# Two cross-attention layers: the order in which a score tile's readers follow each other, and value rows and Gram matrix read back from memory

## The chip, the cores and the metric

One core of a Trainium2 chip runs the whole kernel. The metric is the device time of one execution in microseconds. The core has a matrix engine (TensorE), a vector engine (VectorE), an activation engine (ScalarE), a general engine (GpSimd) and a queue that issues transfers (SyncE); in the profile they are PE (PEld for weight loads), DVE, ACT, POOL and SP. Each engine works through its own instructions in order, and engines wait for each other through semaphores.

## The reference

Two layers of cross-attention follow each other, each with a residual. x is 64 x 256 x 320, the context 64 x 77 x 512; there are 20 heads of 16 channels.

```python
# layer 0: 77 text tokens (the image part is empty)
q, k, v = heads(x @ Wq.T), heads(ctx @ Wk.T), heads(ctx @ Wv.T)
x = merge(softmax(q @ k.T / 4) @ v) @ Wo.T + bo + x

# layer 1: 73 text tokens, and the last 4 as image tokens
q, k_t, v_t = heads(x @ W_q), heads(text @ W_k), heads(text @ W_v)
probs_t = softmax(q @ k_t.T / 4)
text_out = probs_t @ v_t
qsem = l2norm(probs_t @ text)                 # 512 wide
sem = qsem @ l2norm(ip).T
probs_ip = softmax(q @ k_ip.T / 4 + 0.5 * sem) * spatial_mask
x = (text_out + probs_ip @ v_ip) @ W_out + b_out + x
```

## The kernel before, in words

Everything is float32. Channels lie on the partitions for x, queries and outputs; tokens of x lie on the partitions for scores. A pair p of batches (32 pairs) is the unit of projections and outputs. The attention of one layer and one pair is cut into ten units: for each of the two batches b five units of 8 heads by 128 tokens (`UNITS`). One iteration g of the main loop handles one unit of layer 0 (pair p = g // 10, kind k = g % 10), and one unit of layer 1 that lies 13 iterations back (`LAG`), so that layer 1 of pair p - 1 runs with layer 0 of pair p. The loop runs for 345 iterations; layer 0 ends with g = 319.

**The scores' tile.** `sc` takes four of the eight PSUM banks and has one buffer. In each iteration TensorE writes three things into it: the semantic products of a layer 1 unit (`semantics`, L774 and L781), the scores of the layer 0 unit and the scores of the next layer 1 unit (`scores`, L659). The semantic products multiply the unnormalised layer 1 weights with a block of columns: the Gram matrix of the context (77 columns), the value columns and a column of ones. So one product gives, per head, the dot products with the context that norm and image similarity need, the text output and the sum of the weights.

Readers of `sc` in an iteration: VectorE takes the maximum of each head's scores (L677) and the difference to it (L679), for layer 0 and then layer 1 (`shifted`); VectorE multiplies the Gram part with the weights (`weighted`, L792 and L795), whose sum (L1130) is the squared norm; ScalarE copies the last columns out (`sums_out`, L1057). The next iteration's `semantics` waits until all have read.

**What follows.** ScalarE takes the exponentials: layer 0 in L687 (`exponential(0)`), layer 1 in L690 and L691, which go to the tile `parts`. For layer 0, VectorE sums (L705) and inverts, and GpSimd multiplies (L710, tile `parts`). In the next iteration TensorE transposes both layers' weights (`transposed`, L723, L724; tile `tr`, two buffers for all of them, with `itr` and `ltr`), and ScalarE copies the transposes out: L730, L731 for layer 1; L749, L750, or L738, L741 for the last four heads, for layer 0. Layer 1's copies feed the next `semantics`; layer 0's feed the value products `attend` (L809, L814), after units 1 and 4 of a batch.

**Fillers.** `fillers(k, p)` lays the other work between these steps, by kind of iteration: projections of queries (`queries`, L547, L557; copied by L602), keys (`keys`, L345; copied by L348), value rows (`value_rows`, L390), output projections (`project`, L547, L557, added by VectorE in L617; `project_last`, L632, L636), the Gram matrix (`gram`, L512), the image weights' transposes (`image_transposed`, L915) and the outputs' transposes (`outputs`, L928, L940). They share the two buffers of tile `ms`. The list `first` lies between layer 1's and layer 0's transposes, `second` and `third` behind the iteration's vector work. `keep_order` keeps the order of the program on TensorE, VectorE, ScalarE and GpSimd throughout, and on SyncE for the first 13 iterations.

**The order in an iteration.** Scores; maxima and differences; image maximum (`middle`); transposes of layer 1 with their copies; exponential of layer 0 (for k = 5 later); `first`; the product; transposes of layer 0; the sums' copy (for k = 1 and 6 ahead of those transposes); exponentials of layer 1; normalising. For k = 2 `first` lies ahead of the product.

**Values and Gram.** `value_rows(i, l)` makes 128 rows of values of layer l; ScalarE copies them to `vs`, whose two layers go to a tile in memory with one transfer. `values(l, p, b)` reads a batch's rows back, piece by piece where they straddle row tiles: the first 64 tokens twice (`vm`), the remaining 13 or 9 eight times (`vr`, `v_rest`). `place_values` puts them on GpSimd into the block of columns (`gv`, `gr`), for layer 1 with 6 copies and 8 masked products. `gram` copies the Gram matrix from PSUM with two ScalarE copies, scales two parts on GpSimd, and doubles it with one transfer and eight small ones from SBUF to SBUF (L521, L525); `place_gram` spreads it into `gv` and `gr`.

**Tail.** After the last unit of layer 0, `keep_busy` lets TensorE make products that nobody reads (L759), 14 in most iterations with a layer 1 unit.

Of the kernel before, what the change touches and what calls it, by code (L numbers as in the profile page):

```python
# [31 lines left out]
QR = 32  # L32
SLOTS = H + 4
# [37 lines left out]
def tile_two_cross_attentions(ctx: ExitStack, tc: tile.TileContext, a: dict, out: bass.AP):  # L71
# [190 lines left out]
    for sign in (1, -1):  # L262
        nc.gpsimd.affine_select(
            out=rest1, in_=rest1, pattern=[[-sign * QR, 4], [-sign * R1, 2]], compare_op=ALU.is_ge,
            fill=0.0, base=0 if sign > 0 else R1 - 1, channel_multiplier=sign,
        )
# [20 lines left out]
    v_rest = [const.tile([P, C], F32, tag=f"v_rest{b}", name=f"v_rest{b}") for b in range(2)]  # L287
    g_rest = [const.tile([P, R0], F32, tag=f"g_rest{b}", name=f"g_rest{b}") for b in range(2)]
    for t in (*v_rest, *g_rest):
        nc.vector.memset(t, 0.0)  # L290
# [6 lines left out]
    v_rows = {}  # L297
# [83 lines left out]
    stage = {}  # L381

    def value_rows(i, l):

        n = min(P, NB * T - i * P)
        if l == 0:
            stage[i] = sp.tile([P, 2, C], F32, tag="vs", name=f"vs{i}", bufs=1)
        ps = pms.tile([P, 512], F32, tag="ms", name=f"v_ps{l}_{i}")
        for k in range(KE):
            nc.tensor.matmul(ps[:n, :C], cfs[i][:, k, :n], wv[l][:, k, :], start=(k == 0), stop=(k == KE - 1))  # L390
        nc.scalar.copy(stage[i][:n, l, :], ps[:n, :C])
        if l:
            v_rows[i] = dram.tile([P, 2, C], F32, tag="v_rows", name=f"v_rows{i}", bufs=8)
            nc.sync.dma_start(v_rows[i][:n], stage[i][:n])
            if (i + 2) * P < NB * T:
                load_rows(i + 2)

    def from_rows(to, l, p, b, t0, t1):

        r0 = (2 * p + b) * T  # L400
        at, end = r0 + t0, r0 + t1
        while at < end:
            i, r = divmod(at, P)
            n = min(P - r, end - at)
            o = at - r0 - t0
            nc.sync.dma_start(to[o : o + n, :], v_rows[i][r : r + n, l, :])
            at += n
# [5 lines left out]
    def values(l, p, b):  # L413

        nt = (T, TT)[l]
        rem = nt - M
        vm = small.tile([P, C], F32, tag="vm", name=f"vm{l}_{p}_{b}", bufs=1)
        vr = v_rest[b] if l else small.tile([8 * rem, C], F32, tag="vr", name=f"vr{p}_{b}", bufs=1)
        for e in range(2):
            from_rows(vm[e * M : (e + 1) * M, :], l, p, b, 0, M)  # L420
        for i in range(8):
            r = i // 2 * QR + i % 2 * rem if l else i * rem
            from_rows(vr[r : r + rem, :], l, p, b, M, nt)
        fetched[l] = (vm, vr)

    def place_values(l, p, b):
# [3 lines left out]
        if l:  # L430

            for j in range(2):
                rows = slice(j * M, (j + 1) * M)
                for part in range(2):
                    nc.gpsimd.tensor_copy(
                        gv[b][rows, part, :, T : T + D].rearrange("p (e a) d -> p e a d", e=2),
                        vm[rows, 8 * D * part : 8 * D * (part + 1)].rearrange(
                            "p (a j e d) -> p j e a d", a=2, j=2, e=2
                        )[:, j],
                    )  # L440
                nc.gpsimd.tensor_copy(
                    gv[b][rows, 2, :, T : T + D].rearrange("p (e a) d -> p e a d", e=2),
                    vm[rows, HT * D + j * QR : HT * D + (j + 1) * QR]
                    .rearrange("p (e d) -> p e d", e=2).unsqueeze(2).broadcast_to([M, 2, 2, D]),
                )
            for r in range(4):
                rows = slice(r * QR, (r + 1) * QR)
                full = [QR, 2, 2, D]
                nc.gpsimd.tensor_tensor(
                    gr[b][rows, :2, :, T - M : T - M + D],  # L450
                    vr[rows, : HT * D].rearrange("p (i r e d) -> p r i e d", i=2, r=4, e=2)[:, r],
                    rest1[rows].unsqueeze(1).unsqueeze(3).broadcast_to(full), ALU.mult,
                )
                c0 = HT * D + r % 2 * QR
                nc.gpsimd.tensor_tensor(
                    gr[b][rows, 2, :, T - M : T - M + D], vr[rows, c0 : c0 + QR].rearrange("p (e d) -> p e d", e=2),
                    rest1[rows].unsqueeze(2).broadcast_to([QR, 2, D]), ALU.mult,
                )
            return
# [41 lines left out]
    grams = {}  # L501

    def gram(p, b):

        ct = cts[p]
        ps = pms.tile([P, 512], F32, tag="ms", name=f"g_ps{p}_{b}")  # L510
        for k in range(KE):
            nc.tensor.matmul(ps[:TT, :T], ct[:, k, b, :TT], ct[:, k, b, :], start=(k == 0), stop=(k == KE - 1))  # L512
        r = rip[:TT, (2 * p + b) * NIP : (2 * p + b + 1) * NIP]
        g = small.tile([P, T], F32, tag="gram", name=f"gram{p}_{b}", bufs=2)
        rows = small.tile([TT, R0], F32, tag="gram_rest", name=f"gram_rest{p}_{b}", bufs=2)
        nc.scalar.copy(g[:M, :M], ps[:M, :M])
        nc.scalar.copy(rows, ps[:TT, M:T])
        nc.gpsimd.tensor_mul(rows[:, R1:], rows[:, R1:], r)
        nc.gpsimd.tensor_scalar_mul(g[:M, M:TT], rows[:M, :R1], 2.0)
        nc.gpsimd.tensor_copy(g[:M, TT:], rows[:M, R1:])  # L520
        nc.sync.dma_start(g[M:, :], g[:M, :])  # L521
        gx = g_rest[b]
        for i in range(8):
            r0 = i // 2 * QR + i % 2 * R1
            nc.sync.dma_start(gx[r0 : r0 + R1, :], rows[M:TT, :])  # L525
        grams[b] = g

    def place_gram(b):
        g, gx = grams[b], g_rest[b]
# [166 lines left out]
    def rests(two):  # L696

        r = two[:, 4].rearrange("p j (a c) -> p (j a) c", c=QR)
        return r[:, :, : 2 * R1].rearrange("p r (e t) -> p r e t", e=2)
# [252 lines left out]
    def fillers(k, p):  # L952
# [18 lines left out]
        elif k == 1:  # L971
# [5 lines left out]
            add(1, p - 1, place_gram, 0)  # L977
            add(1, p, keys_by_head, 0, p, 1)
            add(1, p - 1, keys_by_head, 1, p - 1, 0)
        elif k == 2:  # L980
# [6 lines left out]
            add(2, p - 1, lambda: made["q"]())  # L987
            add(1, p - 1, place_values, 1, p - 1, 0)
# [21 lines left out]
        elif k == 6:  # L1010
# [9 lines left out]
            add(1, p, place_image_keys, p)  # L1020
            for b in range(2):
# [39 lines left out]
    for g in range(NP * NU + LAG + 12):  # L1061
# [22 lines left out]
        ends = before1 and before1[2] == BU - 1  # L1084
        for l in range(2):
# [11 lines left out]
        if k == 2:  # L1097
            for fn, args in first:
                fn(*args)
        if before1:  # L1100
            prod = weighted(ps, *before1[:4])
        if k != 2:
            for fn, args in first:
                fn(*args)
        if before1 and k in (1, 6):
            sums_out(ps)
# [3 lines left out]
        if idle > 2:  # L1110
            keep_busy(14 if now[1] else {13: 12, 14: 16, 15: 14, 16: 16, 17: 16}.get(idle, 0))
# [6 lines left out]
        if before1 and k not in (1, 6):  # L1118
            sums_out(ps)
# [84 lines left out]
```

## Time and profile before

| | |
|---|---|
| median of three runs | 2474.95 us (2473.02 to 2475.86) |
| the profiled execution | 2474.45 us, span 2472.7 us |
| granted TensorE clock, mean | 0.999 |
| busy: TensorE, VectorE, ScalarE, GpSimd | 97%, 80%, 60%, 55% |
| chain that ended last: TensorE, VectorE, ScalarE, transfers, GpSimd | 76%, 12%, 3%, 3%, 2% |
| layer 0 maximum, difference (each of 320) | 796 and 800 ns |
| layer 1 maximum, difference (each of 320) | 756 and 800 ns |
| product, both parts (each of 320) | 681 and 223 ns |
| sums' copy (each of 320) | 301 ns |
| exponential of layer 0 (each of 320) | 719 ns |
| one pair in the middle, k = 0 to k = 0 | 72.8 us (1179.42 to 1252.23) |

A row of the time line has the start, the duration, the engine, the line and operation, output and inputs, how many instructions are merged in it, and in brackets the idle time just before with what ended it. A row of the waits says which engine at which line waited for whom: total, times, longest. Instructions on one engine overlap a little in their recorded times, so the time from a start to the next start is often less than the duration.

### The profile page before, as it was taken

The page shows a single profiled execution, that of the slowest core. Times are in us where ns is not written, and L with a number is a line of the kernel's source. Part 1 is how long each engine was busy: PE and PEld are TensorE (multiplying, and loading weights), DVE is VectorE, ACT ScalarE, POOL GpSimd, SP SyncE. Part 2 cuts the span into 40 slices and gives each one's busy share as a digit, 9 for nine tenths or more (in the row PEclk, how much of TensorE's full clock was granted, in tenths as well). Part 3 has the DMA queues.
Part 4 walks back from the last instruction along what each step waited for, and adds up shares of the span by engine and source line. Part 5 has one row for each costly group of instructions (what it writes and reads, how often), then busy time and mean ns, then how long its engine had stood idle before and what let it go on. Part 6 is the DMA issues. An engine that isn't in the chain of part 4 may idle for free.

```text
span 2472.7 us, 100470 instructions
## 1 busy us (share of the span) xinstructions
PE 2394.2 (97%) x41118; PEld 1847.9 (75%) x41118; DVE 1987.4 (80%) x3673; ACT 1482.2 (60%) x3767; POOL 1370.9 (55%) x3483
## 2 busy tenths in 40 slices
PE   7899999999999999999999999999999999999888
PEld 5677777777777777777777777777777777777676
DVE  3588788888888888888888888888888888888864
ACT  3466666666666666666665666665665666666543
POOL 2455565566555656555656555556555556555542
PEclk9999999999999999999999999999999999999999
DMA  6212111112111112111121211121211121211000
GB/s 173 75 30 57 50 52 47 56 53 58 52 57 41 54 54 59 52 52 51 47 59 56 62 45 48 46 60 56 62 44 48 47 59 56 61 39 39 26 23 25
DMA packets 150914, 131.83 MB, mean 53 GB/s; under 512 B 45432, under 2 KB 129144, under 8 KB 150456
## 3 DMA queue, kind: packets, MB, share of 16 engines
q1 hardware_dynamic: 149592, 124.27, 17.5%
q8 instruction: 325, 5.32, 0.9%
q10 hardware_dynamic: 864, 1.15, 0.2%
q14 instruction: 133, 1.09, 0.1%
HBM read 87.43 MB, written 33.91 MB: 49 GB/s over the span
## 4 chain that ended last, share of the span: by engine, by line
PE 76%; DVE 12%; ACT 3%; DMA 3%; POOL 2%; issue 1%; SPq 1%; DVEq 0%; POOLq 0%; ACTq 0%
PE tr L723 10%; PE sc L774 9%; PE o_ps L547 8%; PE q_ps L547 8%; PE sc L659 7%; DVE w L679 5%; PE v_ps L390 4%; PE sc L781 4%; PE o_ps L632 3%; DVE mx L677 3%; PE k_ps L345 3%; PE pv L809 2%; PE q_ps L557 2%; PE o_ps L557 2%; PE q_ps L575 2%; PE pv L814 2%
## 5 line engine op out<-in xcount | busy, mean ns | idle before, releaser
L677 DVE TENSOR_REDUCE mx<-sc 128x8 f32<-128x584 f32 (+1 forms) x640 | 496.6, 776 | 342.1 <-PE sc L659 339.3
L710 POOL TENSOR_TENSOR parts<-w,sm 128x512 f32<-128x512 f32 (+1 forms) x640 | 440.6, 709 | 437.1 <-DVE sm L706 144.2
L679 DVE TENSOR_TENSOR w<-sc,mx 128x616 f32<-128x616 f32 x640 | 511.8, 800 | 73.0 <-DVE mx L677 1.4
L723 PE MATMUL tr<-ident,parts 128*128 128x128 f32 x2560 | 407.5, 282 | 9.5 <-ACT pt L730 5.6
L730 ACT COPY pt<-tr 128x512 f32<-128x512 f32 x320 | 187.1, 585 | 323.8 <-PE tr L723 318.9
L723 PEld LDWEIGHTS tr<-ident,parts 128*128 128x128 f32 x2560 | 284.2, 140 | 128.6 <-issue 83.1
L687 ACT ACTIVATE w<-w 128x616 f32<-128x616 f32 x320 | 230.1, 719 | 143.7 <-DVE w L679 142.7
L774 PEld LDWEIGHTS sc<-gv,pt 64*64 64x64 f32 x10240 | 233.5, 133 | 105.6 <-ACT sums L1057 52.7
L774 PE MATMUL sc<-gv,pt 64*64 64x94 f32 x10240 | 277.9, 245 | 23.6 <-ACT sums L1057 23.0
L694 POOL COPY att<-w 128x32 f32<-128x32 f32 x320 | 67.0, 209 | 354.6 <-DVE w L679 350.8
L705 DVE TENSOR_REDUCE sm<-w 128x8 f32<-128x616 f32 x320 | 250.9, 784 | 13.9 <-ACT w L687 13.8
L659 PE MATMUL sc<-kbd,q 32*64 32x154 f32 x10240 | 247.7, 293 | 1.1 <-ACT q L602 1.0
L547 PE MATMUL q_ps<-x,wq 128*128 128x256 f32 x1024 | 232.9, 380 | 5.3 <-ACT kT L348 5.3
L547 PE MATMUL o_ps<-aT,wo 128*128 128x256 f32 x1024 | 231.8, 379 | 0.7 <-ACT aT L945 0.7
L1057 ACT COPY sums<-sc 128x168 f32<-128x168 f32 x320 | 96.2, 301 | 225.8 <-DVE prod L795 223.9
L1130 DVE TENSOR_REDUCE nrm<-prod 128x8 f32<-128x584 f32 x320 | 226.7, 709 | 0.3
L792 DVE TENSOR_TENSOR prod<-sc,parts 128x512 f32<-128x512 f32 x320 | 217.9, 681 | 2.8 <-PE sc L781 2.8
L547 PEld LDWEIGHTS q_ps<-x,wq 128*128 128x128 f32 x1024 | 189.2, 190 | 30.2 <-ACT kT L348 7.3
L547 PEld LDWEIGHTS o_ps<-aT,wo 128*128 128x128 f32 x1024 | 189.6, 190 | 24.4 <-ACT aT L945 1.1
L690 ACT ACTIVATE parts<-w 128x512 f32<-128x512 f32 x320 | 206.4, 645 | 0.0
L749 ACT COPY pt<-tr 128x512 f32<-128x512 f32 x256 | 150.3, 587 | 66.9 <-PE tr L723 65.5
L390 PE MATMUL v_ps<-wv,cf 128*128 128x320 f32 (+1 forms) x624 | 179.2, 433 | 0.0
(144 smaller groups left out, 4560.3 us busy)
## 6 DMA issues: line engine op xcount, KB each, us to landing
out_dram<-x SPq DMA_DIRECT2D x64, 256.0 KB
x<-in_x_dram SPq DMA_DIRECT2D x31, 512.0 KB
v_rows<-vs SPq DMA_DIRECT2D x38, 320.0 KB
vm<-v_rows SPq DMA_DIRECT2D x152, 80.0 KB
ct<-in_ctx_dram SPq DMA_DIRECT2D x32, 308.0 KB
cf<-in_ctx_dram SPq DMA_DIRECT2D x38, 256.0 KB
g_rest<-gram_rest SPq DMA_DIRECT2D x512, 0.5 KB
v_rest<-v_rows SPq DMA_DIRECT2D x448, 11.2 KB
```

What stands on the lines that cost most here:

```text
L390: nc.tensor.matmul(ps[:n, :C], cfs[i][:, k, :n], wv[l][:, k, :], start=(k == 0), stop=(k == KE - 1))
L547: nc.tensor.matmul(ps[b][:, m, :], w[:, k, m * P : (m + 1) * P], main[:, k, b * S : (b + 1) * S], start=(k == 0 and m == 0), stop=False,)
L659: nc.tensor.matmul(ps[c, r, 2 * T * l : 2 * T * (l + 1)], tokens[rows, c], kbd[rows, part].rearrange("p e t -> p (e t)"), start=start, sto ...
L677: nc.vector.tensor_reduce(mx, sc[:, :, :, :nt], AX.X, ALU.max)
L679: nc.vector.tensor_tensor(w, sc, mx.unsqueeze(3).broadcast_to([P, 4, 2, T]), ALU.subtract)
L687: nc.scalar.activation(w, w, AF.Exp, scale=SCALE)
L705: nc.vector.tensor_reduce(sm, w, AX.X, ALU.add)
L710: nc.gpsimd.tensor_tensor(two[:, 8 * t0 : 8 * t1].rearrange("p (h t) -> p h t", h=8), w[:, :, t0:t1], sm.unsqueeze(2).broadcast_to([P, 8, ...
L723: nc.tensor.transpose(ps[:, i, :], flat[:, i * P : (i + 1) * P], ident)
L774: nc.tensor.matmul(ps[c, i % 2 * 2 + j, at : at + GV], pt[half_rows, i, c], gv[b][half_rows, part, i, :], start=start and i < 2, stop=False,)
L792: nc.vector.tensor_tensor(prod[:, :, :, :M], sm[:, :, :, :M], w[:, :4].rearrange("p (e a) j t -> p (a j) e t", e=2), ALU.mult)
L1130: nc.vector.tensor_reduce(eight(stats[q, b][2], u), prod, AX.X, ALU.add)
```

## The change

Three things. First, in each iteration the product and then the sums' copy come ahead of the maxima, with no exceptions by kind left; `first` follows the layer 0 exponential for every k. Second, the value rows go to two tables in memory, one for each layer, from which broadcast transfers read the repeated rows; layer 1's table holds the columns in the order in which `gv` and `gr` want them, so that placing takes one copy and one product; its remaining rows are read in slots of 16 tokens in place of 9, with the mask `rest1` and the layout `rests` changed to match. The Gram matrix goes to memory and comes back by two broadcast transfers (`gram_out`), and `place_gram` of batch 0 moves from k = 1 to k = 2. Third, 8 unread products in place of 14 in the tail.

```diff
+ER = QR // 2
...
     def value_rows(i, l):
...
+        rows = sp.tile([P, (C, 4 * 3 * QR)[l]], F32, tag=f"vs{l}", name=f"vs{l}_{i}", bufs=1)
+        if l == 0:
+            nc.scalar.copy(rows[:n], ps[:n, :C])
+            nc.sync.dma_start(v0_rows[r0 : r0 + n], rows[:n])
+            return
+        to = rows[:n].rearrange("p (r i c) -> p r i c", r=4, i=3)
+        nc.scalar.copy(
+            to[:, :, :2].rearrange("p r i c -> p i r c"), ps[:n, : 2 * P].rearrange("p (i r c) -> p i r c", i=2, r=4)
+        )
+        nc.scalar.copy(
+            to[:, :, 2].rearrange("p (s r) c -> p s r c", s=2),
+            ps[:n, 2 * P : C].rearrange("p (r c) -> p r c", r=2).unsqueeze(1).broadcast_to([n, 2, 2, QR]),
+        )
+        nc.sync.dma_start(v1_rows[r0 : r0 + n], rows[:n])
...
     def values(l, p, b):
...
+            for j in range(2):
+                nc.sync.dma_start(
+                    vm[j * M : (j + 1) * M].rearrange("p a i e d -> p a (i e d)"), rows[r0 : r0 + M, j::2]
+                )
+            for r in range(4):
+                src = rows[r0 + M : r0 + M + ER, r].unsqueeze(0)
+                nc.sync.dma_start(
+                    vr[r * QR : (r + 1) * QR].rearrange("p i c -> p (i c)"), src.broadcast_to([2, ER, 3 * QR])
+                )
+        else:
...
+            for to, t0, t1, n in ((vm, 0, M, 2), (vr, M, T, 8)):
+                src = v0_rows[r0 + t0 : r0 + t1].unsqueeze(0)
+                nc.sync.dma_start(to, src.broadcast_to([n, t1 - t0, C]))
...
     def place_values(l, p, b):
...
+            nc.gpsimd.tensor_copy(
+                gv[b][:, :, :, T : T + D].rearrange("p i (e a) d -> p i e a d", e=2),
+                vm.rearrange("p a i e d -> p i e a d"),
+            )
+            nc.gpsimd.tensor_tensor(
+                gr[b][:, :, :, T - M : T - M + D], vr.rearrange("p i (e d) -> p i e d", e=2),
+                rest1.unsqueeze(1).unsqueeze(3).broadcast_to([P, 3, 2, D]), ALU.mult,
+            )
...
     def gram(p, b):
...
-        nc.scalar.copy(g[:M, :M], ps[:M, :M])
-        nc.scalar.copy(rows, ps[:TT, M:T])
-        nc.gpsimd.tensor_mul(rows[:, R1:], rows[:, R1:], r)
-        nc.gpsimd.tensor_scalar_mul(g[:M, M:TT], rows[:M, :R1], 2.0)
-        nc.gpsimd.tensor_copy(g[:M, TT:], rows[:M, R1:])
-        nc.sync.dma_start(g[M:, :], g[:M, :])
-        gx = g_rest[b]
-        for i in range(8):
-            r0 = i // 2 * QR + i % 2 * R1
-            nc.sync.dma_start(gx[r0 : r0 + R1, :], rows[M:TT, :])
+        nc.scalar.copy(g, ps[:TT, :T])
+        nc.gpsimd.tensor_mul(g[:, TT:], g[:, TT:], r)
+        nc.gpsimd.tensor_scalar_mul(g[:M, M:TT], g[:M, M:TT], 2.0)
+        nc.sync.dma_start(gram_rows[b][:TT], g)
+
+    def gram_out(b):
+        rows = gram_rows[b]
+        nc.sync.dma_start(gram_main[b], rows[:M].unsqueeze(0).broadcast_to([2, M, T]))
+        nc.sync.dma_start(g_rest[b], rows[M:, M:].unsqueeze(0).broadcast_to([8, ER, R0]))
...
             add(0, p - 1, project, 0, p - 1)
-            add(1, p - 1, place_gram, 0)
+            add(0, p - 1, gram_out, 0)
...
         ends = before1 and before1[2] == BU - 1
+        if before1:
+            prod = weighted(ps, *before1[:4])
+            sums_out(ps)
         for l in range(2):
             if now[l]:
                 shifted(ps, l, *now[l])
...
         if now[0] and k != 5:
             exponential(0, g, *now[0])
-        if k == 2:
-            for fn, args in first:
-                fn(*args)
-        if before1:
-            prod = weighted(ps, *before1[:4])
-        if k != 2:
-            for fn, args in first:
-                fn(*args)
-        if before1 and k in (1, 6):
-            sums_out(ps)
+        for fn, args in first:
+            fn(*args)
         if last0:
             transposed(0, *last0)
         idle = g - NP * NU
         if idle > 2:
-            keep_busy(14 if now[1] else {13: 12, 14: 16, 15: 14, 16: 16, 17: 16}.get(idle, 0))
+            keep_busy(8 if now[1] else {13: 12, 14: 16, 15: 14, 16: 16, 17: 16}.get(idle, 0))
...
-        if before1 and k not in (1, 6):
-            sums_out(ps)
```

`gram_out` of batch 1 is called in `first` of k = 6; its `place_gram` stays at k = 8.

## The prediction

> **What bounds the kernel now.** I read the page's head first, then the waits, then the time line of one pair engine by engine. An iteration has ten kinds, k = 0 to 9, one pair of batches long.
>
> ```profile
> span 2472.7 us, 100470 instructions
> PE 2394.2 (97%) x41118; PEld 1847.9 (75%) x41118; DVE 1987.4 (80%) x3673; ACT 1482.2 (60%) x3767; POOL 1370.9 (55%) x3483
> ```
>
> TensorE is the bound, so a change pays only by shortening its gaps (78 us in all) and costs by making new ones.
>
> ```profile
> DVE mx L677 <- PE sc L659: 339.3, 221, 14.5
> ...
> ACT sums L1057 <- DVE prod L795: 223.9, 243, 3.4
> ...
> PE sc L774 <- ACT sums L1057: 23.0, 55, 1.6
> ...
> PEld itr L915 <- ACT pt L749: 4.9, 21, 1.1
> ```
>
> The columns are total, times, longest. The next scores wait for ScalarE's copy of the sums (L1057), the last reader of the scores' tile, in 55 iterations and for 23.0 us: that is all that the order on `sc` costs now. The last row shows another place where the margin is already nil: the image weights' transposes need the buffer that ScalarE's copy L749 empties.
>
> An iteration with k = 2, on three engines:
>
> ```profile
> 1194.86 0.76 PE L659 MATMUL sc<-kbd,q 32*64 32x154 f32 x32
> ...
> 1199.41 0.64 PE L809 MATMUL pv<-pt,v 128*32 128x256 f32 x8
> ...
> 1201.00 0.88 PE L774 MATMUL sc<-gv,pt 64*64 64x94 f32 x32
> ```
> ```profile
> 1194.31 1.65 DVE L617 SCALAR_TENSOR_TENSOR x<-o_ps,bo,x 128x256 f32<-128x256 f32 x4
> 1195.88 0.79 DVE L677 TENSOR_REDUCE mx<-sc 128x8 f32<-128x616 f32 x1
> 1196.70 0.80 DVE L679 TENSOR_TENSOR w<-sc,mx 128x616 f32<-128x616 f32 x1
> ...
> 1199.41 0.68 DVE L792 TENSOR_TENSOR prod<-sc,parts 128x512 f32<-128x512 f32 x1
> 1200.01 0.22 DVE L795 TENSOR_TENSOR prod<-sc,parts 128x72 f32<-128x72 f32 x1
> ```
> ```profile
> 1196.30 0.59 ACT L730 COPY pt<-tr 128x512 f32<-128x512 f32 x1 [1.57 <-PE tr L723]
> ...
> 1197.59 0.72 ACT L687 ACTIVATE w<-w 128x616 f32<-128x616 f32 x1 [0.54 <-DVE w L679]
> 1198.39 0.58 ACT L749 COPY pt<-tr 128x512 f32<-128x512 f32 x1
> 1198.87 0.27 ACT L750 COPY pr<-rtr 104x128 f32<-104x128 f32 x1
> 1200.27 0.30 ACT L1057 COPY sums<-sc 128x168 f32<-128x168 f32 x1 [1.12 <-DVE prod L795]
> ```
>
> ScalarE's queue is in program order: layer 1's transposes (L730), layer 0's exponential (L687), layer 0's transposes (L749, L750), which TensorE needs at 1199.41. L750 ends at 1199.14, so the slack is 0.27 us.
>
> **The new order on `sc`.** In the changed program the product still waits for the last score matmul, not for the semantic ones alone. The sums' copy waits for the product, and layer 0's maximum waits for that copy. So before the maximum now stand the product (0.83 us from its start to the next instruction, e.g. 1223.09 to 1223.91 in the k = 5 iteration), a hand-over of 0.03, the copy 0.30, and a hand-over back that I take as 0.05 (0.04 is seen after this copy at L870): 1.21 us. Queued on ScalarE behind the copy are L730, L687, the fillers' copies, L749; behind the exponential stands everything that TensorE's second half waits for.
>
> The time from the last score to the next scores hardly moves: 4.51 us before (1219.78 to 1224.29), now 0.08 + 1.21 + 3.31 (maximum to second difference) + 0.05 = 4.65. The expensive thing is that the exponential comes 1.2 us later, and more where VectorE comes late to the iteration.
>
> The page "PSUM — Partial Sum Buffer" (Terms) of the Trainium skill says that two engines must not be on one bank at once, two reads included. The row that bears on it is L1057's 223.9 us of waiting for L795, though both only read. By that rule the copy can't lie beside the maximum, and the sum below stays at 182 us; were it allowed, 0.35 us would come off at five places 30 times, which leaves about 130.
>
> **The ten iterations**, with this pair's clock times; where TensorE waits it starts the next iteration later by that much, and VectorE and ScalarE catch up.
>
> - k = 0: VectorE leaves L617 at 1182.75 (1182.21 before; the copy's bubble in k = 9 made it late). Product to 1183.5, sums to 1183.85, maximum from 1183.9, difference ends 1185.6 (+1.70), exponential to 1186.4, the Gram copy 0.2, then L738 (0.58) to 1187.15. Half of L809's second group needs it, at 1185.9 before: **+1.3**.
> - k = 2: L617 ends 1196.55, product 1197.38, sums 1197.72, maximum from 1197.77, difference ends 1199.47, L687 to 1200.2, L749 to 1200.8; L809 starts 1200.85, not 1199.41: **+1.45**.
> - k = 4: L348 (key copy, behind the exponential) at 1215.6 holds the second half of L547 (buffer), due 1215.45: **+0.15**.
> - k = 5: the exponentials of k = 4 end 1217.2, not 1216.7; two table loads of 1.28, two activations and the query copies (L602, 1.05) then end at 1221.6, not 1220.98. The sums' copy stands behind them: to 1221.9, maximum 1221.95, second difference 1225.26, scores at 1225.3, not 1224.29: **+1.0**.
> - k = 6: 1230.66, not 1230.77, since the image maximum (L890, 0.22) now lies behind the differences: **-0.1**.
> - k = 7: VectorE free at 1233.15, sums to 1234.3, difference 1235.98, exponential 1236.7, key copy 0.2, L749 to 1237.4: L915 at 1237.45, not 1235.74: **+1.7**.
> - k = 8: the value copies behind the exponential end 1243.5 and L749 at 1244.05; the outputs' transposes (L928) wait twice, together **+0.65**, where one row tile is left to k = 8 (about 24 pairs of 30).
> - k = 1, 3, 9: TensorE's 3.6 us of projections or queries (L547) cover it: 0. Without that cover k = 3 would lose what k = 2 loses.
>
> The second layer starts in pair 1 at k = 5, so k = 0, 2, 4, 7 count 30 times and k = 5, 6 31 times: 30 x (1.3 + 1.45 + 0.15 + 1.7) = 138; 31 x 0.9 = 28; 24 x 0.65 = 16. Together 182 us.
>
> **The other parts.**
> - The 8 products: 60 fewer, 0.125 each (14 in 1.75 us). In the tail L730's copy, on which they wait, comes about 0.55 later (sums ahead of it), and 0.75 less product makes up for it; both tracks meet at about 2410.8, as now: +2 for the whole tail.
> - GpSimd: the 14 placing instructions per batch took 73.2 + 59.5 + 52.8 + 30.7 = 216 us in all. The two new ones lie between 0.209 (128x32 copy) and 0.961 (128x924), and between 0.317 (128x78 product) and 0.442 (128x154); by size I take 0.35 and 0.34, 44 us. TensorE's waits for GpSimd's parts are 3.9 us, so this is worth 0 (at best -4).
> - ScalarE: the Gram copy is one of 0.2 for two of 0.19 and 0.16; layer 1's rows take two copies (0.37 + 0.27, from 128x256 and 128x128 rows) for one of 0.42. Both are in the sums above.
> - Transfers: the Gram costs 3 issues for 9, values 2 to 6 for 10 and more. Eight issues took 2.79 us of SP, so some 1,400 fewer free about 490 us of a queue that TensorE waits for only at the start (7.1 and 0.8 us): 0. The two trips through memory follow each other: a read behind its write waited at most 3.1 us (`v_rows`), so about 7 us with issues, against 16 us from the Gram copy (1186.5) to where GpSimd places it (k = 2, after 1201). Behind the waiting read on SP stand the value reads and the next x, needed at 1213.6. Bounds: 0, or 1 us of GpSimd per pair, 30 us, if the trips take twice that and the parts behind the placing come late. I take 0.
>
> Profiled execution 2474.45 (span 2472.7 plus 1.75 around it; the median of the runs is 0.5 above): 2474.45 + 182 + 2 = 2658, and with the median's 0.5 I say **2660**.
>
> **Rivals.**
> - Hidden, and faster: TensorE has other work in every iteration, the copies come in time, and only the 23.0 us of L774's waits go: 2452. For it speaks 97% busy; against it the 0.27 us of slack at L809 and L915's row. It decides if the exponential's delay stays under those slacks.
> - Only the loop: the exponential's delay is covered but the loop is 0.14 longer in the two short iterations: 62 x 0.14 = +9, 2484. Against it the same slacks.
> - The clock: the new gaps lower TensorE's granted clock. From 2350 to 2357, after small matmuls and a gap of 1.05, it fell to 0.85 and 0.53, and L774 took 1.53 instead of 0.88. One such dip per pair, about 2.2 us, gives 30 x 2.2 = 66 more: 2726. Against: a gap of 2.14 at 2327 left it at 1.00. The page "TensorE: Matmul & The Clock Gate" of the Trainium skill (What's actually happening) lowers the clock only after an idle window of about 3.4 us, which no gap here fills, so by it this rival adds nothing; the dip above after a gap of 1.05 doesn't fit it.
>
> **Numbers.** Stalls as summed 0.73, with clock dips 0.12, loop only 0.07 (of it 0.02 within 0.2%), hidden 0.08. The five places k = 0, 2, 5, 7, 8 err together if the exponential's delay is mis-sized: 0.6 us less at each, 30 times, is 90 off, 2570; the sum with the clock and half the Gram's bound is 2741. Range 2560 to 2750. About 0.2% can be told from no change here: faster 0.08, same 0.02, slower 0.90.
>
> **What would show it.** A new wait of the maximum for the sums' copy, about 0.4 us in each of some 300 iterations; TensorE's L774 waiting for VectorE's difference and no longer for the sums; new TensorE waits for ScalarE's transposed copies at the value product (30 times about 1.4), the image transposes (30 times 1.7), and the outputs. TensorE's busy time stays within 10 us. Wrong if TensorE's idle time does not grow beyond 150 us, if the maximum follows the product without a gap, or if the waits sit on transfers or GpSimd instead.

## The result, and the profile after

The changed kernel takes 2637.66 us (median of four runs, 2631.95 to 2638.99) against 2474.39: the ratio is 1.0655, 95% interval 1.0637 to 1.0674. It is slower by about 163 us; 2660 was forecast, with 2560 to 2750 as the range.

The head of the changed kernel's page, and the first line of its chain of work that ended last:

```profile
span 2637.3 us, 97894 instructions
...
PE 2411.1 (91%) x41058; PEld 1845.3 (70%) x41058; DVE 2011.8 (76%) x3673; ACT 1479.3 (56%) x3742; POOL 1207.6 (46%) x2651
...
DVE 48%; PE 35%; ACT 10%; issue 5%; DMA 1%; POOL 0%; DVEq 0%; ACTq 0%; SPq 0%; POOLq 0%
```

TensorE's idle time is 226 us (2637.3 - 2411.1), where it was 78: 148 of the 165 us by which the span grew. The chain has changed hands, from TensorE 76% to VectorE 48%, although VectorE is busy for a smaller share than before. So no engine got much more work (VectorE's busy time grew by 24 us, TensorE's by 17); the order of the work makes TensorE wait.

The waits of the changed kernel (total us, times, longest). The new line numbers run some ten lower: the maximum is L667, the sums' copy L1048, semantics L763, layer 1's copied transposes L719, layer 0's L738, value products L798, image transposes L904, the Gram product L505 and its copy L508.

```profile
DVE mx L667 <- ACT sums L1048: 141.6, 318, 1.7
...
PE tr L712 <- ACT pt L719: 43.9, 96, 2.7
...
PE pv L798 <- ACT gram L508: 33.4, 29, 1.2
...
PE sc L763 <- DVE w L669: 24.3, 56, 1.2
...
PE itr L904 <- ACT pt L738: 24.0, 30, 1.6
PE g_ps L505 <- DVE x L607: 23.9, 30, 1.1
...
PE pv L798 <- ACT pt L738: 19.5, 31, 0.8
...
PE atr L917 <- ACT vs L405: 11.0, 23, 0.5
```

The first row is VectorE's: the maximum waits for the sums' copy in 318 iterations, 0.45 us each. The others are TensorE's own, 180 us together. Next scores that waited for the sums have become next scores that wait for VectorE's difference, 55 times then and 56 now, with the same 23 to 24 us. The rest is new, but for 6 waits at the layer 0 transposes. All but one of the new rows of TensorE (L505) end in ScalarE's queue, though ScalarE is busy for only 56% of the span.

An iteration with k = 2, in the changed kernel, on VectorE, ScalarE and TensorE (start, duration, what it is, in brackets the idle time before it and what ended it):

```profile
1273.33 0.22 DVE L784 TENSOR_TENSOR prod<-sc,parts 128x72 f32<-128x72 f32 x1
1273.97 0.80 DVE L667 TENSOR_REDUCE mx<-sc 128x8 f32<-128x616 f32 x1 [0.42 <-ACT sums L1048]
1274.81 0.80 DVE L669 TENSOR_TENSOR w<-sc,mx 128x616 f32<-128x616 f32 x1
```
```profile
1273.64 0.30 ACT L1048 COPY sums<-sc 128x168 f32<-128x168 f32 x1 [2.34 <-DVE prod L784]
1273.83 0.59 ACT L719 COPY pt<-tr 128x512 f32<-128x512 f32 x1
...
1275.70 0.72 ACT L677 ACTIVATE w<-w 128x616 f32<-128x616 f32 x1 [1.10 <-DVE w L669]
1276.32 0.57 ACT L738 COPY pt<-tr 128x512 f32<-128x512 f32 x1
```
```profile
1274.57 0.63 PE L712 MATMUL tr<-ident,parts 128*128 128x128 f32 x4 [0.35 <-ACT pt L719]
...
1276.94 0.64 PE L798 MATMUL pv<-pt,v 128*32 128x256 f32 x8 [0.62 <-ACT pt L738]
```

Read it in order of time. The sums' copy waits 2.34 us at the head of ScalarE's queue for the product. Layer 1's copy L719 stands behind it, and TensorE's next transposes need the buffer that L719 empties: 0.35 us lost. The maximum waits for the same sums' copy, so the exponential L677 starts late; L738 stands behind that, and the value product loses another 0.62. The product began at 1272.73 and the maximum at 1273.97: 1.24 us, where 1.21 was taken.

The change of the time from one iteration's scores to the next, against the kernel before (median over 29 pairs, us):

| k | 0 | 1 | 2 | 3 | 4 | 5 | 6 | 7 | 8 | 9 |
|---|---|---|---|---|---|---|---|---|---|---|
| forecast | 1.3 | 0 | 1.45 | 0 | 0.15 | 1.0 | -0.1 | 1.7 | 0.65 | 0 |
| measured | 1.88 | 0 | 1.09 | 0 | 0.43 | 0.31 | -0.01 | 1.42 | 0.76 | -0.23 |

The 29 pairs lose 154 us in all, the last pair 9.2, start and tail 1.5: 165.

### The profile page after: what moved, and what is told of

Read it like the earlier page. It is cut to its first block, busy times and chain, and to the rows that moved or that the text cites. A ratio compares the mean times of both kernels' runs of the same rounds, so it can differ in the third digit from the quotient of the medians.

```text
span 2637.3 us, 97894 instructions
## 1 busy us (share of the span) xinstructions
PE 2411.1 (91%) x41058; PEld 1845.3 (70%) x41058; DVE 2011.8 (76%) x3673; ACT 1479.3 (56%) x3742; POOL 1207.6 (46%) x2651
## 3 DMA queue, kind: packets, MB, share of 16 engines
q10 hardware_dynamic: 864, 1.15, 0.1%
## 4 chain that ended last, share of the span: by engine, by line
DVE 48%; PE 35%; ACT 10%; issue 5%; DMA 1%; POOL 0%; DVEq 0%; ACTq 0%; SPq 0%; POOLq 0%
DVE w L669 13%; DVE mx L667 12%; DVE prod L781 6%; PE sc L763 5%; PE q_ps L537 5%; PE sc L649 4%; DVE sm L694 4%; DVE x L607 3%; DVE nrm L1114 3%; ACT sums L1048 3%; PE pv L798 3%; PE v_ps L395 2%; PE tr L712 2%; PE pv L803 2%; PE sc L770 2%
## 5 line engine op out<-in xcount | busy, mean ns | idle before, releaser
L667 DVE TENSOR_REDUCE mx<-sc 128x8 f32<-128x584 f32 (+1 forms) x640 | 497.7, 778 | 179.2 <-ACT sums L1048 141.6
L712 PE MATMUL tr<-ident,parts 128*128 128x128 f32 x2560 | 409.8, 283 | 48.5 <-ACT pt L719 43.9
L677 ACT ACTIVATE w<-w 128x616 f32<-128x616 f32 x320 | 229.8, 718 | 340.5 <-DVE w L669 340.5
L712 PEld LDWEIGHTS tr<-ident,parts 128*128 128x128 f32 x2560 | 278.7, 141 | 185.9 <-issue 95.2
L1048 ACT COPY sums<-sc 128x168 f32<-128x168 f32 x320 | 96.1, 300 | 487.4 <-DVE prod L784 486.7
L763 PEld LDWEIGHTS sc<-gv,pt 64*64 64x64 f32 x10240 | 236.5, 134 | 98.3 <-DVE w L669 45.4
L763 PE MATMUL sc<-gv,pt 64*64 64x94 f32 x10240 | 277.4, 245 | 25.1 <-DVE w L669 24.3
L719 ACT COPY pt<-tr 128x512 f32<-128x512 f32 x320 | 189.7, 593 | 0.8 <-PE tr L712 0.7
L738 ACT COPY pt<-tr 128x512 f32<-128x512 f32 x256 | 150.2, 587 | 50.1 <-PE tr L712 50.1
```

The costliest lines, as they stand in the source:

```text
L667: nc.vector.tensor_reduce(mx, sc[:, :, :, :nt], AX.X, ALU.max)
L677: nc.scalar.activation(w, w, AF.Exp, scale=SCALE)
L712: nc.tensor.transpose(ps[:, i, :], flat[:, i * P : (i + 1) * P], ident)
L763: nc.tensor.matmul(ps[c, i % 2 * 2 + j, at : at + GV], pt[half_rows, i, c], gv[b][half_rows, part, i, :], start=start and i < 2, stop=False,)
```

## The experiments

**The two halves of the change apart.** The first experiment keeps the new tables and Gram transfers, with the old order in the loop and 14 unread products.

```diff
-        if before1:
-            prod = weighted(ps, *before1[:4])
-            sums_out(ps)
...
+        if k == 2:
+            for fn, args in first:
+                fn(*args)
+        if before1:
+            prod = weighted(ps, *before1[:4])
...
+        if before1 and k not in (1, 6):
+            sums_out(ps)
```

> The changed kernel with the old order of product, sums' copy, fillers and maxima, and 14 unread products: only the value tables, the Gram through memory and the fewer placing instructions are left of the change. Theory (the whole loss comes from the order on the scores' tile, by way of the layer 0 exponential's place in ScalarE's queue): 2474 us, at most 5 off, since the placing, the transfers and the Gram's trips are covered. Rival (part of the 163 us comes from the Gram's two trips through memory or from the transfers): 2500 us or more, with GpSimd waiting for a transfer ahead of the placing. Rival on the other side (the freed GpSimd time or SyncE issues shorten TensorE's gaps): 2470 or less.

Measured: 2463.49 us, ratio 0.9952 (0.9939 to 0.9964), faster than the theory's 2474 less 5, where its second rival had it. The second is the reverse: the kernel before, with the new order and the 8 products.

```diff
+        if before1:
+            prod = weighted(ps, *before1[:4])
+            sums_out(ps)
         for l in range(2):
```

> The kernel before with the new order and 8 unread products alone; values and Gram move as before. Theory (the order is all): 2638 us, within 8. Rival (the transfers carry half of the loss): about 2555. If this and the run with the data part alone add up to the whole change, the parts are independent.

Measured: 2643.34 us, ratio 1.0672 (1.0658 to 1.0687). The order alone makes the whole loss, and a little more; the tables and the Gram matrix's way through memory are a gain of about half a per cent that the order hides.

**Where the half per cent comes from.** In the kernel before, some iterations with k = 4 took 9.7 us in place of 8.2. One of them, on GpSimd, in SyncE's queue, on ScalarE and on TensorE:

```profile
771.67 0.72 POOL L464 TENSOR_TENSOR v<-vm,half 128x320 f32<-128x320 f32 x1 [4.78 <-DMA vm<-v_rows]
```
```profile
763.95 7.85 SPq L406 DMA_DIRECT2D v_rest<-v_rows  x8
772.42 1.10 SPq L406 DMA_DIRECT2D vm<-v_rows  x2
```
```profile
774.03 0.28 ACT L348 COPY kT<-k_ps 128x146 f32<-128x146 f32 x1 [2.32 <-POOL kbd L376]
```
```profile
774.36 1.99 PE L547 MATMUL q_ps<-x,wq 128*128 128x256 f32 x8 [1.28 <-ACT kT L348]
```

Layer 0's values come late, GpSimd waits 4.78 us for them, the key block behind them on GpSimd is late, ScalarE's key copy waits for it, and TensorE loses 1.28 us; SyncE had just spent 7.85 us on eight small issues. In the first experiment GpSimd's waits for `vm` fall from 26.0 us (8 times) to 7.5 (3 times), the five TensorE waits at the queries are gone, and the k = 4 iterations of pairs 2 to 30 take 6.1 us less in all. Of the 11.6 us by which the two spans differ, another 4.1 come ahead of pair 2.

The ninth experiment takes the Gram matrix back to the old way in the first one, to divide the gain.

```diff
-        nc.sync.dma_start(gram_rows[b][:TT], g)
+        nc.sync.dma_start(g[M:, :], g[:M, :])
+        gx = g_rest[b]
+        for i in range(8):
+            r0 = i // 2 * QR + i % 2 * ER
+            nc.sync.dma_start(gx[r0 : r0 + R1, :], rows[M:TT, :])
...
-            add(0, p - 1, gram_out, 0)
+            add(1, p - 1, place_gram, 0)
```

> The run with the data part alone, but with the Gram moved as before the change (nine transfers inside SBUF, two ScalarE copies, placed at k = 1 for batch 0). Theory (the 12 us that the data part gains come from the value reads: fewer issues ahead of layer 0's value read on SyncE, for which GpSimd waited 26 us in 8 places): 2464 us, within 3. Rival (the Gram's eight small transfers are the crowd on SyncE): 2472 or more.

Measured: 2467.74 us, ratio 0.9964 (0.9950 to 0.9978). That is just above the expected range (2464, within 3). The k = 4 gain (5.9 us) is all there, so it belongs to the values. What the Gram transfers add, some 4 us between the medians, is not told apart: the two intervals overlap.

**The sums' copy or the product?** The third experiment leaves the product ahead of the maximum and puts the sums' copy back behind layer 0's transposes.

```diff
             prod = weighted(ps, *before1[:4])
-            sums_out(ps)
...
+        if before1 and k in (1, 6):
+            sums_out(ps)
...
+        if before1 and k not in (1, 6):
+            sums_out(ps)
```

> The changed kernel with the product ahead of the maxima but the sums' copy where it was before (late, for k = 1 and 6 ahead of layer 0's transposes). The maximum no longer waits for ScalarE; the exponential of layer 0 comes 0.83 us late and not 1.25, and layer 1's transposes are no longer copied behind the sums. Theory (the loss grows with the exponential's delay beyond each place's slack): about 2545 us, 2520 to 2580, TensorE's waits for L719's copy of layer 1 gone, those for the layer 0 copies smaller by some 0.4 us each. Rival (the product's place alone does it): 2630 or more. Rival (the copy's place alone does it): 2480 or less.

Measured: 2505.01 us, ratio 1.0119 (1.0105 to 1.0132). 133 of the 163 us go with the copy's place; the product alone, 0.82 us on VectorE, leaves the kernel 30 us slower than before, and 44 slower than the same with the old order (2461.23, below). It was expected to cost more (2520 at the least): k = 2 is back to +0.08, k = 0 to +0.64 and k = 7 to +0.59. TensorE's waits in this kernel:

```profile
PE itr L904 <- ACT pt L738: 22.5, 30, 1.7
PE pv L798 <- ACT gram L508: 18.4, 29, 0.6
PE sc L763 <- ACT sums L1048: 16.9, 38, 1.6
PE tr L712 <- ACT pt L719: 6.4, 6, 2.1
```

The 96 waits at L712 are down to 6: the copy at the head of ScalarE's queue had made them. The image transposes still wait as long as in the changed kernel; they hang on the exponential.

**Two ways from the sums' copy to TensorE.** The fourth experiment cuts the one through the exponential: it leaves the changed kernel as it is and puts layer 0's exponential behind the copies of layer 0's transposes for k = 0, 2, 7 and 8 too, as k = 5 has it.

```diff
-        if now[0] and k != 5:
+        if now[0] and k not in (0, 2, 5, 7, 8):
             exponential(0, g, *now[0])
...
-        if now[0] and k == 5:
+        if now[0] and k in (0, 2, 5, 7, 8):
```

> The changed kernel with layer 0's exponential behind the copies of layer 0's transposes also for k = 0, 2, 7 and 8 (as it is for k = 5); product and sums' copy stay ahead of the maxima. Theory (TensorE waits for copies that stand behind the exponential on ScalarE): the waits at the value product, the image transposes and the outputs go (1.15 at k = 0, 0.62 at k = 2, 0.77 at k = 7, 0.5 at k = 8, some 90 us in all); what stays are 0.78 at k = 0 for the vector engine, 0.35 and 0.9 for the copies of layer 1's transposes, 0.3 at k = 5: about 2550 us, 2525 to 2580. Rival (VectorE's chain, 48% of the chain of waits, is the bound and the queue's order doesn't matter): 2620 or more.

Measured: 2563.61 us, ratio 1.0356 (1.0341 to 1.0372). The waits of this kernel:

```profile
DVE mx L667 <- ACT sums L1048: 141.3, 318, 1.7
PE tr L712 <- ACT pt L719: 47.2, 96, 2.7
...
PE sc L763 <- DVE w L669: 24.7, 57, 1.2
PE g_ps L505 <- DVE x L607: 23.8, 30, 1.1
PE o_ps L622 <- DVE x L607: 10.2, 31, 1.4
```

The rows of L798 and L904 are gone, 77 us together in the changed kernel, and the time falls by 74. The maximum waits as before, so these 74 us came not from that wait itself but from what stands behind it on ScalarE. What is left are L712's waits for layer 1's copy, and waits for VectorE. The two figures agree in sum, not place by place: k = 0, 7 and 8 gain, but k = 2 loses as much as in the changed kernel (table below). Where its wait at the value product went, it waits longer at L712 (0.49 us for 0.36) and newly for VectorE's additions (0.26 at L622, 0.30 at L574). One such k = 2 of this kernel:

```profile
1237.26 1.52 PE L622 MATMUL o_ps<-aT,wo 128*64 128x256 f32 x12 [0.26 <-DVE x L607]
1239.26 0.63 PE L712 MATMUL tr<-ident,parts 128*128 128x128 f32 x4 [0.49 <-ACT pt L719]
```

The eighth experiment cuts the other way: VectorE copies the sums itself, so that nothing on ScalarE stands behind that copy, while the maximum comes as late as the copy makes it.

```diff
-        nc.scalar.copy(eight(stats[before1[:2]][1], before1[2]), by_block(ps)[:, :, :, TT:])
+        nc.vector.tensor_copy(eight(stats[before1[:2]][1], before1[2]), by_block(ps)[:, :, :, TT:])
```

> The changed kernel with the sums copied out by VectorE itself, between the product and the maximum, in place of ScalarE. ScalarE's queue is free for layer 1's transposes as before the change; the maximum still waits for a copy of about 0.27 us, some 0.15 us less than the hand-over to ScalarE and back. Theory (the exponential's delay sets the loss; TensorE's waits for the layer 1 copies only stand ahead of waits for layer 0's copies that come anyway): 2595 us, 2580 to 2612, the waits for L719 gone and those at the value product and the image transposes longer than before by what TensorE comes earlier. Rival (layer 1's copies queued behind the sums' copy are a loss of their own, 44 us): 2570 or less.

Measured: 2556.08 us, ratio 1.0321 (1.0307 to 1.0335), below the theory's range and where the rival had it. On VectorE in this kernel, and its waits:

```profile
1261.98 0.22 DVE L784 TENSOR_TENSOR prod<-sc,parts 128x72 f32<-128x72 f32 x1
1262.12 0.32 DVE L1048 COPY sums<-sc 128x168 f32<-128x168 f32 x1
1262.36 0.79 DVE L667 TENSOR_REDUCE mx<-sc 128x8 f32<-128x616 f32 x1
```
```profile
PE itr L904 <- ACT pt L738: 37.2, 30, 2.3
PE pv L798 <- ACT gram L508: 25.4, 29, 0.9
...
PE tr L712 <- ACT pt L719: 7.1, 6, 2.5
```

From the product's second part to the maximum it is 0.38 us here (1261.98 to 1262.36) and 0.64 in the changed kernel (1273.33 to 1273.97): two hand-overs between engines cost 0.26 more than copying on the engine that waits. L712's waits are back to 6, L904's have grown. By kind of iteration, against the kernel before (medians over 29 pairs, us):

| k | 0 | 1 | 2 | 3 | 4 | 5 | 6 | 7 | 8 | 9 |
|---|---|---|---|---|---|---|---|---|---|---|
| changed kernel | 1.88 | 0 | 1.09 | 0 | 0.43 | 0.31 | -0.01 | 1.42 | 0.76 | -0.23 |
| third experiment | 0.64 | 0 | 0.08 | 0 | 0 | 0 | -0.23 | 0.59 | 0.24 | 0 |
| fourth | 0.71 | 0 | 1.22 | 0 | 0.43 | 0.31 | -0.01 | 0.57 | 0 | -0.23 |
| eighth | 1.36 | 0 | 0.57 | 0 | 0.09 | -0.09 | -0.25 | 1.15 | 0.49 | -0.23 |

Of the 165 us by which the span grew, 84 stay with the first cut and 82 with the second. That the cuts save about the same does not show that the two ways cost the same, since the second cut also brings the maximum, and with it the exponential, 0.26 us forward. That alone helps: k = 6 and 8 have no wait at L712 in the changed kernel, and gain 0.24 and 0.27. And k = 7, where 0.60 us at L712 go, gains no more than 0.27, since its wait at L904 grows from 0.77 to 1.29.

An estimate from these runs: from the third experiment to the eighth the maximum comes 0.24 later, with ScalarE's queue free for layer 1's copies in both, and the 29 pairs lose 49 us, 203 for each microsecond of delay. From the changed kernel to the fifth experiment (next) it comes 0.33 later, and they lose 81, 245 for each. At these rates 0.26 make 53 to 64 of the 71 us that the second cut saves in the 29 pairs. What is left for layer 1's copies in the queue is 8 to 19 us; no run measures it by itself.

**Twice the copy.** The fifth experiment calls the sums' copy twice in the changed kernel.

```diff
             sums_out(ps)
+            sums_out(ps)
```

> The changed kernel with the sums' copy made twice in a row on ScalarE (the second writes the same values). From the start of one copy to the next instruction behind it are 0.20 us, so the maximum, and with it the exponential, come 0.20 us later than in the changed kernel. Theory (every place where TensorE already waits, k = 0, 2, 4, 5, 7, 8, loses the added delay in full, since no slack is left there): 6 x 30 x 0.20 = 36 more, 2675 us, 2660 to 2690. Rival (the maximum's wait for the copy is hidden, the loss has another cause): 2640 or less.

Measured: 2725.72 us, ratio 1.1003 (1.0988 to 1.1018), 88 us over the changed kernel where 37 were expected. The waits of this kernel:

```profile
DVE mx L667 <- ACT sums L1048: 246.4, 318, 2.0
PE tr L712 <- ACT pt L719: 92.7, 156, 3.0
```

The direction is as the theory has it, the size is not. The second copy was priced by the distance of two starts on ScalarE (0.20); it delays the maximum by 0.33 ((246.4 - 141.6) / 318). Of that, k = 1 and 9 still hide all and k = 3 half (+0.15); k = 4 to 8 lose 0.27 to 0.34, so nothing is left there to hide it; k = 0 and 2, where TensorE waits twice, lose 0.66 and 0.60. L712 waits 60 times more.

**The order where it might help.** The seventh experiment puts the product alone ahead, for k = 6 and in the tail (from g = 320), on top of the first one, with 8 unread products.

```diff
+        ahead = k == 6 or g >= NP * NU
+        if before1 and ahead:
+            prod = weighted(ps, *before1[:4])
...
-        if before1:
+        if before1 and not ahead:
             prod = weighted(ps, *before1[:4])
```

> The data part of the change with the old order, except that for k = 6 and in the tail (no layer 0 unit any more) the product comes ahead of the maxima, with the sums' copy where it was, and 8 unread products. Theory (the product ahead costs only where a layer 0 copy with too little slack stands behind the exponential; k = 6 gained 0.22 us an iteration and the tail 4 us with the product alone ahead): 2463 less 7 less 4, 2453 us, 2449 to 2457, the fastest of all. Rival (those gains were recovered waits of iterations before, not gains of their own): 2463.

Measured: 2460.54 us, ratio 0.9935 (0.9923 to 0.9948). The time lies above the theory's range: k = 6 gains 5.1 us over the 29 pairs and k = 7 gives 6.0 back, as the rival had it. The tail gains 5.8 and the last pair loses 2.2, and it was open whether by the order or by the products. Two kernels tell that apart: the first experiment with 8 products, and the same with the product ahead in the tail only. A third gives the changed kernel its 14 products back.

```diff
-            keep_busy(14 if now[1] else {13: 12, 14: 16, 15: 14, 16: 16, 17: 16}.get(idle, 0))
+            keep_busy(8 if now[1] else {13: 12, 14: 16, 15: 14, 16: 16, 17: 16}.get(idle, 0))
```

> The kernel of the first experiment (new value and Gram transfers, old order on the scores' tile) with 8 unread products in the tail in place of 14. In the tail of that kernel the unread products stand between layer 1's transposes and the wait for ScalarE's copy of them; theory: there the copy is what ends last, so 6 products fewer (0.75 us in each of some 10 iterations) are hidden or save a little: 2463.5, 2459 to 2465. Rival: the products are the longer track, and all of the 0.75 us comes off about ten times: 2456.

```diff
+        ahead = g >= NP * NU
+        if before1 and ahead:
+            prod = weighted(ps, *before1[:4])
```

> The same with the product ahead of the maximum in the tail only (from g = 320, where layer 0 has ended), the sums' copy where it was, 8 unread products. Theory: the 4 us that the tail lost with this order in two earlier experiments is the order's own, since no layer 0 exponential stands behind it there, and the 2 to 3 us that the last pair lost beside it come from the last iterations with k = 6 and 7: 2459.5, 2457 to 2462, some 4 below the first experiment and 1 below the seventh. Rival: the last pair's loss goes with the tail's gain, so that the sum is nil: 2463.

```diff
-            keep_busy(8 if now[1] else {13: 12, 14: 16, 15: 14, 16: 16, 17: 16}.get(idle, 0))
+            keep_busy(14 if now[1] else {13: 12, 14: 16, 15: 14, 16: 16, 17: 16}.get(idle, 0))
```

> The changed kernel with 14 unread products in the tail in place of 8, all else as it is. Theory: in the tail the product and the sums' copy now stand ahead of what TensorE waits for, and 8 products end before ScalarE's copy does; 14 end after it, so some of 0.75 us a time comes on: 2643, 2638 to 2646. Rival: the clock needs the longer run of products, and 14 are as fast or faster than 8: 2636.

Measured: 2461.23 us (0.9939, 0.9926 to 0.9951), 2460.96 (0.9935, 0.9921 to 0.9948) and 2642.11 (1.0668, 1.0653 to 1.0682). In the one profile of each, the tail takes 3.8 us less than before with fewer products alone, and 5.9 with the order too. But the last pair, whose code is the same in both, takes 0.9 less in the first and 0.7 more in the second. In both the granted clock is halved for two stretches of 3.4 us in last pair and tail; the later one lies in the tail of the first (2440.8) and in the last pair of the second (2336.3). Last pair and tail together gain 4.7 and 5.2, and the medians are 0.3 apart. So the gain is the products', the order adds nothing that these runs show, and the tenth experiment's reason falls, though its time lies in its range. In the changed kernel, 14 products make the tail 5.3 us longer than 8 in the one profile; the median is 4.5 higher, with intervals that overlap. The three kernels with new transfers, old order in the pairs (but for k = 6 in one) and 8 products lie within 0.7 us of each other; the one to keep is the plain one, 2461 us. Its interval overlaps that of the first experiment, but it beats the kernel before by 0.5 to 0.7%.

## Why the prediction was right, and where its sizes were not

**What decides, and its sign.** "The expensive thing is that the exponential comes 1.2 us later" held: with the exponential taken out of the queue's way, 74 of the 163 us went. A second way stands in the prediction as a list ("Queued on ScalarE behind the copy are L730 ...") without a price: layer 1's copies wait at ScalarE behind a sums' copy that waits for VectorE, and TensorE's layer 0 transposes wait for their buffer, 96 times and 43.9 us. In one iteration the two delays partly stand for each other: k = 2 waits 0.36 at L712 and 0.62 at the value product where it loses 1.09, and it loses 1.22 when the second of these waits is gone. What the second way costs by itself is not shown (8 to 19 us by the estimate above). The forecast booked nearly the whole loss to the exponential. That its sum of 182 came out near is partly luck: over 29 pairs k = 0 lost 17 us more than was said, and k = 2, 5 and 7 lost 10, 20 and 9 less.

**Term by term.** The product to the maximum: 1.24 us for 1.21. The maximum's wait: 0.45 in 318 iterations for 0.4 in some 300. The next scores: the sums replaced by the difference, as said, and the loop no longer. k = 8 had 0.76 for 0.65, and nothing in the pairs with two row tiles; k = 1 and 3 had their nothing; the tail had 1.5 for 2.

**k = 0, 1.9 for 1.3.** The wrong copy was taken. TensorE and ScalarE in the changed kernel, k = 0:

```profile
1257.22 0.73 PE L505 MATMUL g_ps<-ct 128*73 128x77 f32 x8 [0.78 <-DVE x L607]
...
1261.24 0.64 PE L798 MATMUL pv<-pt,v 128*32 128x256 f32 x8 [1.15 <-ACT gram L508]
```
```profile
1260.36 0.72 ACT L677 ACTIVATE w<-w 128x616 f32<-128x616 f32 x1 [1.11 <-DVE w L669]
1260.98 0.20 ACT L508 COPY gram<-g_ps 73x77 f32<-73x77 f32 x1
1261.09 0.58 ACT L727 COPY pt<-tr 128x512 f32<-128x512 f32 x1
```

The value product's first group needs the buffer of `ms` that the Gram copy L508 empties, behind the exponential, and waits 1.15 us; the prediction had the second group wait for the transposes' copy (L738, now L727), which comes after. And the Gram product itself waits 0.78 us for VectorE to finish the output projection's addition (L607), which empties the buffer that it takes: VectorE is late from k = 9, which the prediction saw for VectorE (1182.75 for 1182.21) but did not follow to the buffer. k = 9 itself came out 0.23 shorter.

**k = 5, 0.3 for 1.0.** The forecast carried k = 4's late exponentials through two table loads to the query copies. But k = 4 lost 0.43 itself (0.15 was said), 0.24 of it at L712, so k = 5 began later against the same loads; that is read from the rows and was not tried by itself. The two together, 0.74, stand against 1.15.

**k = 2 and k = 7, 1.1 for 1.45 and 1.4 for 1.7.** TensorE had already lost time earlier in the iteration (0.60 at L712 in k = 7), and L915 (now L904) then waits 0.77, not 1.7.

**Not in the sum.** The last pair lost 9.2 us, some 4 more than a pair in the middle: its k = 5 lost 2.7 and its k = 7 lost 3.8. TensorE's idle time grew by 5.6 us there, not much more than in a pair in the middle (5.1). The wait of 2.67 us at one L712 is hardly new: the kernel before has 2.14 in the same place (2327.42). The rest is the clock: it is halved for 6.8 us in that k = 5 and for 6.8 in that k = 7 (last section), where the kernel before has one stretch of 3.4 us in this pair (from 2353.5). TensorE's wait and the granted clock in the last pair of the kernel before:

```profile
2327.42 0.63 PE L723 MATMUL tr<-ident,parts 128*128 128x128 f32 x4 [2.14 <-ACT pt L730]
```
```profile
2353.50:2356.80 3.30, 3.30 (x64) 0.50 0.12 29
```

**"Transfers/SyncE: 0" and GpSimd "at best -4"** had the wrong size: the data half is worth 11 to 13 us in the old order. The five waits of TensorE that it removes stood in the profile of before ("PE q_ps L547 <- ACT kT L348", 5.3 us, 5 times), with the late value read two steps behind them; the forecast looked only for TensorE's direct waits on transfers. In the new order less of it is left: the difference between the second experiment and the changed kernel is 5.7 us, and the intervals of their ratios overlap. GpSimd's placing was right: 22.9 + 22.3 = 45 us, for 44.

**The rivals.** Hidden, or only the loop: both out, by the rows of L712, L798 and L904. The clock: granted in full from 198 us up to the last pair. From there on it was halved for 21 us in all in the changed kernel and for 7 in the kernel before, so this rival has at most half of the difference, 7 us, of the 163. The sign asked for in TensorE's busy time, "within 10 us", did not hold: it rose by 17. The mean granted clock of 0.995 for 0.999 would make about 10 of them (0.4% of 2411); the rest was not traced.

## What to carry to other kernels

When a reader of a shared buffer moves ahead of another engine's reader, price the queue behind it, not the buffer: here TensorE's waits for the buffer's readers hardly changed (23.0 us before, 24.3 now), and nearly all of the 163 us came from two in-order queues, VectorE's and ScalarE's, in which something urgent came to stand behind something that waits. Follow an engine's waits back more than one step before a cost of an off-path transfer is set to nothing. And where a change bundles a good and a bad part, run each alone: the good half of this one is worth keeping.

## What the runs showed of the hardware

A copy in a chain from engine to engine costs more than its place in the queue. A 128x168 copy from PSUM takes 0.30 us on ScalarE and the next one can start 0.20 us after it, but a second one in the chain delayed VectorE by 0.33, and the first costs VectorE a gap of 0.42. The same copy on VectorE takes 0.32 and moves the maximum by 0.24 (1262.12 to 1262.36).

The granted clock of the changed kernel stayed at 1.00 from 198 to 2470 us, with gaps of up to 1.15 us in every pair. It fell in the last pair and the tail. Stretches of 28 us of the changed kernel (TensorE's busy time and instructions, granted clock, share and rate of the transfers), two shorter stretches within them, and TensorE's unread products in the last pair:

```profile
2442.00:2470.00 28.00, 25.08 (x437) 1.00 0.13 39
2470.00:2498.00 28.00, 22.00 (x363) 0.88 0.04 10
2498.00:2526.00 28.00, 21.85 (x357) 0.88 0.04 12
2526.00:2554.00 28.00, 25.02 (x437) 1.00 0.11 32
```
```profile
2486.40:2493.20 6.80, 6.12 (x104) 0.50 0.01 2
...
2503.50:2510.20 6.70, 5.58 (x48) 0.50 0.01 2
```
```profile
2477.86 1.04 PE L748 MATMUL busy<-ident 128*128 128x128 f32 x8
...
2484.96 0.63 PE L712 MATMUL tr<-ident,parts 128*128 128x128 f32 x4 [2.67 <-ACT pt L719]
...
2488.63 1.97 PE L748 MATMUL busy<-ident 128*128 128x128 f32 x8 [0.68 <-ACT gram L508]
```

The same eight products take 1.04 us and, soon after a gap of 2.67 and one of 0.68, 1.97. The page "TensorE: Matmul & The Clock Gate" (What's actually happening) of the Trainium skill lowers the clock after an idle window of about 3.4 us; no single gap here is that long, so the row shows the clock falling after gaps that are shorter. In the traces of all the kernels here, every such dip behind the start and ahead of the end of the span has a clock of 0.50 and lasts 3.41 or 6.83 us. In the 3.41 us ahead of the two dips shown TensorE stood idle for 2.0 and 2.1 us; ahead of the one at 2353.5 in the kernel before it was 1.15, so the idle time alone does not tell when the clock falls. The dips differ from run to run: the four runs of the changed kernel lie 7 us apart, and the one with the least time, 2631.95, had a mean clock of 0.999, the longest, 2638.99, 0.995.
